# Moving the own part's sums of one batch into a spare column tile of the next batch's decay product

## The chip, the cores and the metric

The kernel runs on one core of a Trainium2 chip. The core has five engines that work side by side, each through its own queue in order: TensorE (PE in the profile; its weight loads are PEld), VectorE (DVE), ScalarE (ACT), GpSimd (POOL), and SyncE (SP), which here issues DMAs. TensorE writes into PSUM, which this kernel uses as eight banks of 128 partitions by 512 fp32 values: six tiles named `ps` and one tile of two banks, `wrep`. The metric is the time of one execution on the device in microseconds; the median of three runs is given.

## The reference

The reference is one block of an RWKV-like layer with 8 batches, 256 time steps, 512 channels, 32 heads of 16 channels. Cut to what matters here:

```
xn  = layernorm(x);  sx = previous row of xn - xn
xxx = tanh((xn + sx * maa_x) @ maa_w1)          # five groups of 32 columns
x5[g] = xn + sx * (maa_stack[g] + xxx[g] @ maa_w2[g])
w = exp(-exp(time_decay + tanh(x5[1] @ decay_w1) @ decay_w2))
r, k, v = x5[3] @ Wr.T, x5[0] @ Wk.T, x5[2] @ Wv.T;  g = silu(x5[4] @ Wg.T)
step t:  a = k_t v_t^T                          # per head, 16 x 16
         out_t = r_t (faaaa * a + s);   s = a + w_t * s
att = groupnorm(out) per head;  x = x + (att * g) @ Wo.T
x = x + sigmoid(xr @ ffn_Wr.T) * (square(relu(xk @ ffn_Wk.T)) @ ffn_Wv.T)
```

In `out_t` the term with `faaaa` needs no state: for each head it is v_t times the sum over the head's channels of faaaa * r_t * k_t. The kernel calls this the own part, and the change is about those sums.

## The kernel before, in words

The work of a batch is written in three stages: `inputs_of_scan` (layer norm, the mixes x5, the decay w, the projections k, v, r, g), `scan` (the recurrence and the own part), and `rest` (group norm, output projection, the feed-forward half). Three batches are in flight: while batch b is in its scan, batch b+1 is in its inputs and batch b-1 in its rest.

Activations lie with channels on partitions and time along the row: a tile of [128, 2, 256] holds two blocks of 128 channels, so one batch of 512 channels takes two tiles (index `q`), four blocks in all.

**The decay product (L785 to L802).** `pd` is one PSUM tile. For each of the four blocks k of the contraction, four matmuls run in the four column tiles of 32 of the array. Tiles 0 and 1 take `decay_w1` (64 columns) with x5[1] as the moving operand. Tiles 2 and 3 take the fifth group of `maa_w1` with `xin`; its 32 columns stand twice in the weight, so tile 3 repeats what tile 2 computes. ScalarE then takes tanh of rows 0 to 63 into `hd` (twice, L800) and of rows 64 to 127 into `tb` (twice, L802), since the next product wants that result repeated on all 128 partitions.

**The own part (L864 to L888).** POOL multiplies r by k into two tiles `rk` (L867). Four matmuls, one per block and column tile, sum them per head with the mask `hm`, which holds faaaa (L872), into 4 x 32 rows of a PSUM tile `pc`. ScalarE copies each block's 32 rows of 256 values onto the four quarters of the tile `att`, 16 copies a batch (L880). POOL multiplies `att` by v (L886).

**The scan (L882 to L936).** For each of the four blocks: DMAs bring v spread over the partitions (`vs`), DVE multiplies by k (L917) and runs the scan (L919), POOL multiplies by r (L922), and a gather of 16 matmul calls on PE (L930) sums over the head's channels into a PSUM tile `pat`. DVE adds `pat` to `att` (L936).

**The other names in the text.** `mul` at L400 issues nearly all other products; a product whose form is "any" runs as four narrow matmuls (128 x 32 of the array) or one wide one (128 x 128), after the form that stood last on PE. L612 is the turn by identity, L754 and L668 additions of POOL in the mixes, L900 the decays for the scan, L989 the copies of the group norm's factors, which take one of the two `rk` tiles for the second half.

**What sets the order.** Every operation is added to a plan with an engine, an estimated time, its tiles and a number. The numbers stand in the long table `TURNS` (from L121), one row a stage: the plan takes the ready operation with the lowest number, gives it a tile of its pool when one comes free, and each engine's queue follows the result. Pools bound the lookahead: six `ps` tiles in PSUM, two `rk`, three `att`, three each of k, r, v, w.

Of the kernel before, what the change touches and what calls it, by code (L numbers as in the profile page):

```python
# [9 lines left out]
AF = mybir.ActivationFunctionType  # L10
ALU = mybir.AluOpType
# [56 lines left out]
class Plan:  # L68
# [46 lines left out]
    def stage(self):  # L115
# [224 lines left out]
def tile_rwkv_block(  # L340
# [357 lines left out]
    def inputs_of_scan(b, got):  # L698
# [102 lines left out]
        for rows in (slice(0, 64), slice(64, 128)):  # L801
            act(T, tb, [pd], lambda rows=rows: nc.scalar.activation(tb()[rows, :], pd()[64:128, 0, :], AF.Tanh), "exp")  # L802
# [354 lines left out]
```

## Time and profile before

| what | value |
|---|---|
| runs, median (lowest to highest) | 609.45 us (609.26 to 609.94) |
| profiled execution, span from first to last instruction | 607.3 us |
| instructions in the trace | 17606 |
| mean granted TensorE clock | 1.000 |
| activation table loads | 43, of 1283 ns each |
| DMA, mean | 205 GB/s |

The profile gives the profiled execution's span, not its device time. The time of a run is about 2 us longer than the span (609.45 - 607.3 = 2.15). A row such as `L872 PE MATMUL ps<-rk,hm 128*32 128x256 f32 x64` reads: line, engine, operation, output from inputs, the form of the array (contraction rows * columns of one tile), the output's shape and type, and the count. An fp32 matmul call appears as two records.

### The profile page before, as it was taken

The page shows a single profiled execution, that of the slowest core. Times are in us where ns is not written, and L with a number is a line of the kernel's source. Part 1 is how long each engine was busy: PE and PEld are TensorE (multiplying, and loading weights), DVE is VectorE, ACT ScalarE, POOL GpSimd, SP SyncE. Part 2 cuts the span into 40 slices and gives each one's busy share as a digit, 9 for nine tenths or more (in the row PEclk, how much of TensorE's full clock was granted, in tenths as well). Part 3 has the DMA queues.
Part 4 walks back from the last instruction along what each step waited for, and adds up shares of the span by engine and source line. Part 5 has one row for each costly group of instructions (what it writes and reads, how often), then busy time and mean ns, then how long its engine had stood idle before and what let it go on. Part 6 is the DMA issues. An engine that isn't in the chain of part 4 may idle for free.

```text
span 607.3 us, 17606 instructions
## 1 busy us (share of the span) xinstructions
PE 597.2 (98%) x7270; PEld 344.8 (57%) x7270; DVE 543.9 (90%) x492; ACT 514.6 (85%) x1172; POOL 520.2 (86%) x417
## 2 busy tenths in 40 slices
PE   9999999999999999999999999999999999999997
PEld 7675555467544664377553775455644464446464
DVE  6699999999999998899989999999999999995442
ACT  6878779999999999999999898999989799965450
POOL 2899999999899999899989998999898998898020
PEclk9999999999999999999999999999999999999999
DMA  8798855878778787859767996688659877951542
GB/s 319 224 266 218 232 147 142 227 181 215 220 220 215 219 219 205 213 145 268 198 198 191 277 239 189 186 240 225 188 174 263 203 204 227 258 186 42 175 168 92
DMA packets 52640, 124.77 MB, mean 205 GB/s; under 512 B 5841, under 2 KB 11345, under 8 KB 52561
## 3 DMA queue, kind: packets, MB, share of 16 engines
q1 hardware_dynamic: 48048, 119.39, 71.3%
q10 hardware_dynamic: 4512, 4.26, 2.3%
q8 instruction: 57, 0.93, 0.7%
q14 instruction: 23, 0.18, 0.1%
HBM read 115.25 MB, written 8.39 MB: 204 GB/s over the span
## 4 chain that ended last, share of the span: by engine, by line
PE 78%; POOL 14%; DVE 3%; issue 3%; ACT 1%; DMA 1%; DVEq 0%; POOLq 0%; ACTq 0%
PE ps L400 65%; PE ps L930 8%; POOL st L922 7%; PE ps L612 2%; POOL mix L754 2%; PE ps L794 2%; POOL vs L914 2%; DVE st L919 1%; POOL mix L782 1%; POOL att L886 1%; POOL sx L640 1%; PE ps L956 1%; DMA xt<-in_x 1%; PE ps L872 0%; DVE vs L917 0%
## 5 line engine op out<-in xcount | busy, mean ns | idle before, releaser
L919 DVE TENSOR_TENSOR_SCAN st<-wrep,vs 128x1024 f32<-128x1024 f32 x128 | 288.2, 2277 | 2.9 <-ACT wrep L900 0.8
L922 POOL TENSOR_TENSOR st<-st,r 128x1024 f32<-128x1024 f32 x128 | 254.5, 2005 | 9.3 <-DVE st L919 9.0
L917 DVE TENSOR_TENSOR vs<-vs,ps 128x1024 f32<-128x1024 f32 x122 | 143.7, 1208 | 2.6 <-ACT vs L910 2.4
L400 PE MATMUL ps<-Ws,mix 128*32 128x512 f32 (+3 forms) x872 | 115.2, 586 | 0.1
L400 PEld LDWEIGHTS ps<-Ws,mix 128*32 128x32 f32 (+1 forms) x872 | 37.6, 116 | 63.4 <-issue 56.0
L754 POOL TENSOR_TENSOR mix<-mix,xn 128x512 f32<-128x512 f32 x62 | 66.6, 1098 | 6.9 <-DVE mix L738 5.5
L930 PE MATMUL ps<-st,con 128*32 128x256 f32 x1024 | 62.1, 380 | 0.8 <-POOL st L922 0.7
L400 PE MATMUL ps<-mix,Wv 128*32 128x256 f32 (+1 forms) x832 | 60.5, 380 | 1.6 <-DVE mix L751 0.9
L400 PE MATMUL ps<-mix,Wk 128*32 128x256 f32 (+1 forms) x952 | 59.2, 379 | 0.1
L400 PE MATMUL ps<-mix,Wg 128*32 128x256 f32 (+1 forms) x664 | 58.8, 379 | 0.0
L400 PE MATMUL ps<-mix,Wr 128*32 128x256 f32 (+1 forms) x688 | 58.5, 380 | 0.0
L400 PE MATMUL ps<-mix,Ws 128*32 128x256 f32 (+1 forms) x664 | 57.3, 379 | 0.0
L400 PE MATMUL ps<-Ws,g 128*32 128x512 f32 (+1 forms) x416 | 56.9, 593 | 0.2 <-POOL g L1001 0.2
L736 ACT ACTIVATE ps<-ps,vec 128x256 f32<-128x256 f32 x112 | 47.6, 444 | 3.8 <-PE ps L400 2.3
L880 ACT COPY att<-ps 32x256 f32<-32x256 f32 x128 | 46.6, 364 | 4.4 <-ACT v L825 1.3
L668 POOL TENSOR_TENSOR mix<-mix,xn 128x512 f32<-128x512 f32 x44 | 47.3, 1093 | 3.4 <-ACT mix L666 3.2
L400 PEld LDWEIGHTS ps<-mix,Wv 128*32 128x32 f32 (+1 forms) x832 | 37.7, 116 | 21.2 <-DVE mix L751 1.6
L400 PEld LDWEIGHTS ps<-mix,Ws 128*32 128x32 f32 (+1 forms) x664 | 40.0, 124 | 15.5 <-ACT o L1025 0.5
L400 PEld LDWEIGHTS ps<-mix,Wr 128*32 128x32 f32 (+1 forms) x688 | 39.3, 123 | 16.5 <-issue 1.3
L930 PEld LDWEIGHTS ps<-st,con 128*32 128x32 f32 x1024 | 32.7, 110 | 27.5 <-issue 4.4
L400 PEld LDWEIGHTS ps<-mix,Wg 128*32 128x32 f32 (+1 forms) x664 | 39.9, 124 | 14.8 <-issue 0.7
L400 PEld LDWEIGHTS ps<-mix,Wk 128*32 128x32 f32 (+1 forms) x952 | 35.0, 112 | 22.3 <-issue 2.9
(141 smaller groups left out, 968.1 us busy)
## 6 DMA issues: line engine op xcount, KB each, us to landing
vs<-vo SPq DMA_DIRECT2D x128, 512.0 KB, 5.7
Ws<-in_fk SPq DMA_DIRECT2D x16, 512.0 KB, 6.1
Ws<-in_wo SPq DMA_DIRECT2D x16, 512.0 KB, 6.2
Ws<-in_fr SPq DMA_DIRECT2D x16, 512.0 KB, 6.1
Ws<-in_fv SPq DMA_DIRECT2D x16, 512.0 KB, 5.2
x<-in_x SPq DMA_DIRECT2D x9, 512.0 KB, 8.0
vo<-v ACTq DMA_DIRECT2D x15, 256.0 KB, 5.4
out<-o SPq DMA_DIRECT2D x15, 256.0 KB, 4.9
```

What stands on the lines that cost most here:

```text
L400: nc.tensor.matmul(out[i : i + n], lhsT=w[:, i : i + n], rhs=x, start=first, stop=final)
L612: nc.tensor.transpose(to[:, m, n * P : (n + 1) * P], xh[n]()[:, k * P : (k + 1) * P], idt())
L668: gp(512, t, [t, xn[q]], lambda q=q, t=t: nc.gpsimd.tensor_tensor(t(), t(), xn[q]()[:, :, 1 : T + 1], ALU.add))
L736: act(256, p_, [p_, vec], lambda g=g, q=q, m=m, p_=p_: nc.scalar.activation(p_()[:, m, :], p_()[:, m, :], AF.Identity, bias=col(f"maa_{g}" ...
L754: gp(512, t, [t, xn[q]], lambda q=q, t=t: nc.gpsimd.tensor_tensor(t(), t(), xn[q]()[:, :, 1 : T + 1], ALU.add))
L794: nc.tensor.matmul(pd()[i : i + 32, 0, :], lhsT=w, rhs=src[k // 2]()[:, k % 2, :], start=(k == begin), stop=(k == end))
L880: act(350, atts[q], [pc], lambda i=32 * (2 * q + m), m=m, q=q, h=32 * h: nc.scalar.copy(atts[q]()[h : h + 32, m, :], pc()[i : i + 32, 0, :]))
L914: gp(4 * T, vs, [vs, k], lambda m=m, vs=vs, k=k: nc.gpsimd.tensor_tensor(vs(), vs(), k.place[:, m : m + 1, 1 : T + 1].to_broadcast([P, 4, ...
L917: dve(4 * T, [vs], [vs, kp], lambda m=m, vs=vs, kp=kp: nc.vector.tensor_tensor(vs(), vs(), kp()[:, m : m + 1, :].to_broadcast([P, 4, T]), ...
L919: dve(4 * T, [st], [w, vs], lambda w=w, vs=vs, st=st: nc.vector.tensor_tensor_scan(st().rearrange("p n t -> p (n t)"), w().rearrange("p n ...
L922: gp(4 * T, st, [st, r], lambda m=m, st=st, r=r: nc.gpsimd.tensor_tensor(st(), st(), r()[:, m : m + 1, :].to_broadcast([P, 4, T]), ALU.mul ...
L930: nc.tensor.matmul(pat()[32 * i : 32 * i + 32, 0, :], lhsT=con()[:, s : s + 32], rhs=done[i]()[:, j, :], start=(j == 0), stop=(j == 3),)
```

## The change

1. In every batch but the first, the fourth column tile of the decay product no longer repeats the third. It runs the own part's matmul of the batch before, one block for each step k: blocks 0 and 1 into rows 96 to 127 of `pd` itself, blocks 2 and 3 into the same rows of a second PSUM tile. The separate product of four matmuls remains only for the last batch.
2. As rows 96 to 127 of `pd` no longer hold the repeated part, `tb` is filled by four tanh of 32 rows instead of two of 64.
3. The two blocks of a tile now lie beside each other on the same 32 partitions, so ScalarE copies them at once: 8 copies of 32 x 512 a batch in place of 16 of 32 x 256. The last batch keeps its 16.
4. The two multiplications r * k on POOL are listed at the end of `inputs_of_scan`, as the next batch's inputs need them; the stages are written down in the order inputs of b+1, scan of b, rest of b.
5. All numbers in `TURNS` are new: 2599 operations instead of 2648.

```
     def inputs_of_scan(b, got):
+        own = gots[b - 1] if b else None
...
                 for k in ks:
-                    for i in range(0, P, 32):
+                    for i in range(0, P if b == 0 else 96, 32):
                         w, src = (dw1()[:, k, i : i + 32], x5[1]) if i < DEC else (w1()[:, k, P + i - DEC : P + i - 32], xin)
                         nc.tensor.matmul(
                             pd()[i : i + 32, 0, :], lhsT=w, rhs=src[k // 2]()[:, k % 2, :], start=(k == begin), stop=(k == end))
+                    if own:
+                        nc.tensor.matmul(own["pc"][k // 2]()[96:128, k % 2, :], lhsT=hm()[:, k, :],
+                                         rhs=own["rks"][k // 2]()[:, k % 2, :], start=True, stop=True)
...
+            if own:
+                own["pc"] = [pd, new("ps", f"pc{b - 1}")]
+                pe(0.432 * len(ks), own["pc"], [dw1, w1, hm, *ins, *own["rks"]], mm, "columns", [hd, tb])
+                continue
             pe(0.432 * len(ks), [pd], [dw1, w1, *ins], mm, "columns", [hd, tb])
...
-        for rows in (slice(0, 64), slice(64, 128)):
-            act(T, tb, [pd], lambda rows=rows: nc.scalar.activation(tb()[rows, :], pd()[64:128, 0, :], AF.Tanh), "exp")
+        n = 32 if own else 64
+        for rows in (slice(i, i + n) for i in range(0, P, n)):
+            act(T, tb, [pd], lambda rows=rows: nc.scalar.activation(tb()[rows, :], pd()[64 : 64 + n, 0, :], AF.Tanh), "exp")
...
+        got["rks"] = []
+        for q in range(NQ):
+            r, k, rk = got["r", q], got["k", q], new("rk", f"rk{b}_{q}")
+            gp(512, rk, [r, k], lambda rk=rk, r=r, k=k: nc.gpsimd.tensor_tensor(rk(), r(), k(), ALU.mult))
+            got["rks"].append(rk)
...
     def scan(b, got):
...
+        if b == NB - 1:
...
+        else:
+            for q, pc in enumerate(got["pc"]):
+                for h in range(0, P, 32):
+                    act(610, atts[q], [pc], lambda q=q, h=h, pc=pc: nc.scalar.copy(atts[q]()[h : h + 32], pc()[96:128]))
...
+    gots = [{} for _ in range(NB)]
+    stages = [(inputs_of_scan, 0, 0)]
     for b in range(NB):
+        stages += [(inputs_of_scan, 0, b + 1)] * (b + 1 < NB) + [(scan, 1, b), (rest, 2, b)]
+    for stage, i, b in stages:
+        stage(b, gots[b])
+        phases[b + i].append((i, plan.stage()))
```

The branch for the last batch holds the code of before; the two lines of `rk` that stood in `scan` are gone there. The new table of numbers is left out.

More of the change, by code (lines that the diff above doesn't have):

```diff
@@ L861, in scan, with mm @@
         act(4, cm, [cm], lambda: nc.scalar.mul(cm(), cm(), -1.0 / S))
-        rks, pc = [], new("ps", f"pc{b}")
-        for q in range(NQ):
-            r, k, rk = got["r", q], got["k", q], new("rk", f"rk{b}_{q}")
-            gp(512, rk, [r, k], lambda rk=rk, r=r, k=k: nc.gpsimd.tensor_tensor(rk(), r(), k(), ALU.mult))
-            rks.append(rk)
-        def mm():
-            for i in range(NK):
-                nc.tensor.matmul(
-                    pc()[32 * i : 32 * i + 32, 0, :], lhsT=hm()[:, i, :], rhs=rks[i // 2]()[:, i % 2, :], start=True, stop=True)
-        atts = [new("att", f"att{b}_{q}") for q in range(NQ)]
-        pe(0.437, [pc], [hm, *rks], mm, "columns")
-        for q in range(NQ):
-            for m in range(2):
-                for h in range(4):
-                    act(350, atts[q], [pc], lambda i=32 * (2 * q + m), m=m, q=q, h=32 * h: nc.scalar.copy(
-                        atts[q]()[h : h + 32, m, :], pc()[i : i + 32, 0, :]))
+        atts = [new("att", f"att{b}_{q}") for q in range(NQ)]
+        if b == NB - 1:
+            pc, rks = new("ps", f"pc{b}"), got["rks"]
+            def mm():
+                for i in range(NK):
+                    nc.tensor.matmul(
+                        pc()[32 * i : 32 * i + 32, 0, :], lhsT=hm()[:, i, :], rhs=rks[i // 2]()[:, i % 2, :], start=True, stop=True)
+            pe(0.437, [pc], [hm, *rks], mm, "columns")
+            for q in range(NQ):
+                for m in range(2):
+                    for h in range(4):
+                        act(350, atts[q], [pc], lambda i=32 * (2 * q + m), m=m, q=q, h=32 * h: nc.scalar.copy(
+                            atts[q]()[h : h + 32, m, :], pc()[i : i + 32, 0, :]))
+        else:
+            for q, pc in enumerate(got["pc"]):
+                for h in range(0, P, 32):
+                    act(610, atts[q], [pc], lambda q=q, h=h, pc=pc: nc.scalar.copy(atts[q]()[h : h + 32], pc()[96:128]))
         for blk in range(NK):
@@ L1073, in tile_rwkv_block @@
     phases[0].append((0, plan.stage()))
+    gots = [{} for _ in range(NB)]
+    stages = [(inputs_of_scan, 0, 0)]
     for b in range(NB):
-        got = {}
-        for i, stage in enumerate((inputs_of_scan, scan, rest)):
-            stage(b, got)
-            phases[b + i].append((i, plan.stage()))
+        stages += [(inputs_of_scan, 0, b + 1)] * (b + 1 < NB) + [(scan, 1, b), (rest, 2, b)]
+    for stage, i, b in stages:
+        stage(b, gots[b])
+        phases[b + i].append((i, plan.stage()))
     with tc.manual_schedule():
```

247 rows, old and new, of the table TURNS are left out of this document.

## The prediction, made before the changed kernel was run

> **What bounds the kernel now.** I read the page's busy times first, then its chain of waits in order of time, then the busy time by stretch. On the page every engine is nearly full, with TensorE (PE) first:
>
> ```profile
> PE 597.2 (98%) x7270; PEld 344.8 (57%) x7270; DVE 543.9 (90%) x492; ACT 514.6 (85%) x1172; POOL 520.2 (86%) x417
> ...
> PE 78%; POOL 14%; DVE 3%; issue 3%; ACT 1%; DMA 1%; DVEq 0%; POOLq 0%; ACTq 0%
> ```
>
> A share of busy time is no bound yet. The chain of waits says where which engine sets the end. Its columns are the start, the length, and the engine with its line:
>
> ```profile
> 34.21 2.00 POOL st L922
> ...
> 48.53 1.05 POOL rk L867
> ...
> 140.21 1.97 POOL st L922
> 142.22 1.93 PE ps L930 x32
> 144.15 3.45 PE ps L400 x64
> ...
> 523.91 3.43 PE ps L400 x32
> 527.34 1.80 PE ps L930 x32
> 529.25 2.15 issue
> 531.40 1.20 DVE vs L917
> ```
>
> So there are three parts. From about 34 to 142 us the chain runs through POOL (the ramp, scans of batches 0 and 1). From 142 to 529 us it runs through PE. The end, from 529 us, is the last batch alone. The busy times by stretch agree and add something (columns: length, then PE, PEld, DVE, ACT, POOL, granted clock, DMA share, GB/s):
>
> ```profile
> 52.00:120.00 68.00, 66.26 (x1121) 37.70 (x1116) 66.71 (x56) 58.21 (x128) 67.95 (x47) 1.00 0.75 187
> 120.00:200.00 80.00, 79.66 (x915) 45.07 (x908) 79.65 (x64) 76.42 (x182) 76.86 (x61) 1.00 0.79 208
> ...
> 360.00:440.00 80.00, 79.91 (x984) 46.09 (x987) 78.45 (x66) 73.37 (x174) 74.97 (x60) 1.00 0.75 207
> 440.00:520.00 80.00, 80.00 (x1164) 41.12 (x1160) 77.94 (x63) 71.81 (x153) 72.99 (x53) 1.00 0.81 218
> ```
>
> From 360 to 520 us PE has 0.09 us idle in 160. VectorE (DVE) has 1.55 and 2.06 us of slack per 80, ScalarE (ACT) 6.63 and 8.19. In the first two rows DVE is as full as PE: 1.29 us of slack in 68, 0.35 in 80. So a microsecond of PE work removed after 142 us should shorten the run by a microsecond, as long as DVE loses less than it has in hand; before 142 us it may buy nothing.
>
> The profiled execution has a span of 607.3 us. The page does not give its device time; the median of the runs is 609.45 us, so I take 2.15 us around the span and hold it fixed.
>
> **Part 1: four matmuls go, seven times (a gain).** The own part's product (L872) has four calls, one per column tile, recorded as eight matmuls. What it takes from PE is the distance from its start to the next group's start:
>
> ```profile
> 52.90 0.61 PE L872 MATMUL ps<-rk,hm 128*32 128x256 f32 x8
> 53.33 1.91 PE L930 MATMUL ps<-st,con 128*32 128x256 f32 x32
> ...
> 96.88 0.61 PE L872 MATMUL ps<-rk,hm 128*32 128x256 f32 x8
> ...
> 182.66 0.61 PE L872 MATMUL ps<-rk,hm 128*32 128x256 f32 x8
> ...
> 390.29 0.61 PE L872 MATMUL ps<-rk,hm 128*32 128x256 f32 x8
> 390.72 3.64 PE L400 MATMUL ps<-mix,Wv 128*32 128x256 f32 x64
> ```
>
> The first and the last pair of rows both give 0.43 us. Batch 7 keeps its product, so seven go: 7 x 0.43 = 3.01 us. The same four calls now run in the fourth column tile of the next batch's decay product (L794), in place of the repeated one. Whether that is free depends on whether a tile with another moving operand runs beside the others. The product of before already mixes two moving operands (with weights from dw and from mw):
>
> ```profile
> 60.24 0.39 PE L794 MATMUL ps<-mix,dw 128*32 128x256 f32 x2
> 60.25 0.39 PE L794 MATMUL ps<-mix,mw 128*32 128x256 f32 x2
> 60.46 0.39 PE L794 MATMUL ps<-mix,dw 128*32 128x256 f32 x2
> ```
>
> All four tiles start within 0.01 us, and the next four 0.22 us later. I therefore cost the replacement at nothing. If the new operand or the second output tile broke this, each of the four steps would cost two further slots of 0.22 us, 1.76 us a batch.
>
> The products of batches 0, 1 and 2 start at 52.90, 96.88 and 182.66 us. So five of the seven (batches 2 to 6) lie in the stretch that PE bounds: 5 x 0.43 = 2.15 us, taken in full. Those of batches 0 and 1 lie in the ramp: between 0 and 0.86 us, and I take half, 0.43, since PE is 97% busy there though not on the chain. Together 2.58 us.
>
> **Part 2: changes of array form (a small loss).** Products without a fixed form run wide (128*128) or narrow (128*32), as the last form in the order was. Counting along the new numbers by that rule I get 82 changes of form on PE against 80 before, and 185 narrow products out of 277 against 186. A change is seen here:
>
> ```profile
> 288.45 3.62 PE L400 MATMUL ps<-mix,Wg 128*128 128x256 f32 x16
> 292.00 0.64 PE L872 MATMUL ps<-rk,hm 128*32 128x256 f32 x8
> 292.46 0.83 PE L400 MATMUL ps<-mix,Wg 128*32 128x256 f32 x12
> ```
>
> Sixteen wide matmuls at 0.216 us would let the next start at 291.91; it starts at 292.00, and the eight narrow ones then take 0.46 instead of 0.43. That is 0.12 us a change, 0.2 us for two.
>
> **Part 3: ScalarE (off the path).** The copies of one batch go from 16 of 32x256 to 8 of 32x512, and the tanh into `tb` from two of 64 rows to four of 32:
>
> ```profile
> L880 ACT COPY att<-ps 32x256 f32<-32x256 f32 x128 | 46.6, 364 | 4.4 <-ACT v L825 1.3 <-PE ps L872 1.3
> L825 ACT COPY k<-ps 128x512 f32<-128x512 f32 x16 | 9.3, 581 | 3.1 <-PE ps L400 3.0
> L802 ACT ACTIVATE tb<-ps 64x256 f32<-64x256 f32 x16 | 6.1, 381 | 0.7 <-ACT v L843 0.4
> L855 ACT ACT_TABLE_LOAD x11 | 14.1, 1283 | 0.2
> ```
>
> No copy of 32x512 is in the trace. The 32x256 and 64x256 rows show that row count hardly matters, so I take 0.58 us from the 128x512 row; the bound above is twice the short one, 0.73, at which the copies gain nothing, and below it is 0.36, that of one short copy. A batch saves 16 x 0.364 - 8 x 0.58 - 2 x 0.381 = 0.42 us, seven save 2.9. Along the new numbers I count 46 changes of the activation table against 43, three more at 1.28 us: 3.9 us. ACT ends about 1 us fuller, of 92.7 us idle. It is 1% of the chain, so I enter nothing; if ACT had no room, that 1 us would be the price.
>
> What a table change costs beside its own row is seen here, where the load starts as the copies end and the next activation starts as it ends:
>
> ```profile
> 55.08 1.28 ACT L855 ACT_TABLE_LOAD   x1
> 56.37 0.60 ACT L855 ACTIVATE g<-ps 128x512 f32<-128x512 f32 x1
> ```
>
> [...]
>
> **Part 4: waits and buffers.** The POOL multiplications into `rk` (L867) are as many as before, only listed at the end of the inputs, and by the numbers they stand where they stood, ahead of the same batch's scan; nothing on POOL gets longer. No DMA is moved by the edit itself, though the new numbers shift SP's loads by four places on average, and I enter nothing for that; a load that came late would show as a wait of PE for a DMA.
>
> The decay product now waits for `rk` of the batch before and for a second PSUM tile. Behind it in PE's queue stands all later work, but `rk` is numbered well before it. What comes later is the result: the copies can only start after the decay product. By the numbers that product stands after the first gather (L930) in batches 2 to 6. Until the copies (4 x 0.58 us), POOL's multiplication by v (L886) and DVE's addition (L936) are done, the gathered tile is held, one of six in PSUM. The waits now are small:
>
> ```profile
> DVE att L936 <- POOL att L886: 3.7, 2, 2.7
> ...
> PEld ps L930 <- POOL st L922: 4.3, 9, 0.9
> ```
>
> Against this stands what is freed. The own part's tile is held today until the last of 16 scattered copies:
>
> ```profile
> 225.55 0.61 PE L872 MATMUL ps<-rk,hm 128*32 128x256 f32 x8
> ...
> 264.72 0.36 ACT L880 COPY att<-ps 32x256 f32<-32x256 f32 x1 [0.44 <-ACT v L825]
> ```
>
> That is 39 us for one tile of six; with eight copies that the numbers put close together, two tiles are held for a shorter time. Which side wins I cannot read from the trace. The bounds are the idle PE time that can go, 1.74 + 0.34 = 2.1 us between 52 and 200 us, and new stalls as priced below. I enter zero.
>
> **The sum.** 2.58 - 0.2 = 2.4 us: span 604.9, time 609.45 - 2.4 = 607.1 us. By itself this case spans 606.4 (all seven products count, no cost of form) to 607.5 (only the five count, 2.15 - 0.2). A measurement of this kernel can tell about 0.2%, 1.2 us, so the forecast is a faster kernel.
>
> **Rivals.** *The order also fills the ramp (0.13).* PSUM is freed sooner and PE's 2.1 us of idle time up to 200 us goes: 609.45 - 3.0 - 2.1 = 604.3 us. For it speaks the 39 us hold; against it that the chain in the ramp is POOL's, whose work stays.
>
> *The gain is hidden (0.17).* The ramp keeps its 0.86 us, and one slot of 0.22 us a batch is given back in PE waits for a PSUM tile, 7 x 0.22 = 1.54 us: 2.15 - 0.2 - 1.54 = 0.4 us, time 609.0. For it: DVE at 79.65 of 80 us up to 200 us. Against: nothing but PE is full after 360.
>
> *Own sums come too late, slower (0.13).* Place: DVE's addition L936, in order, in front of scans that POOL and PE wait for. Today it waits 3.7 us in two cases, 1.85 each. If each of the seven batches waited so, that is 13.0 us, 9.3 more. The four stretches quoted hold 1.29 + 0.35 + 1.55 + 2.06 = 5.2 us of DVE slack, so 4.1 us would reach the end: 609.45 + 4.1 - 2.4 = 611.1 us. It decides from 5.2 + 2.4 = 7.6 us of extra waiting, 1.1 us a batch. Against it: the numbers also move the addition behind more scan work, which is what a wait would need.
>
> *The fourth tile does not run beside the others (0.02).* Then the change doesn't do what it says: 7 x 1.76 - 3.0 = 9.3 us more, 618.8 us. The L794 rows speak against it.
>
> **How the numbers follow.** The forecast has 0.55. Faster is 0.55 + 0.13 = 0.68, within 0.2% 0.17, slower 0.13 + 0.02 = 0.15. The range goes from 604.0, just under the first rival, to 609.9, over the hidden gain with four more such slots; the slower rivals and a small part of the first stay outside, under 0.2.
>
> **What would show it.** Right: L872 with 8 matmul records in place of 64, the decay products still 1.7 us long with four tiles starting together, PE busy about 3 us less and as full as now from 142 us on, a 32x512 copy near 0.58 us. Wrong: matmuls of the fourth tile starting 0.2 us behind the others; DVE's wait for L886 far over 3.7 us; more idle PE time in front of L930 or L400 after 142 us; a chain that leaves PE later than 142 us; or a PE busy time down by 3 us with an equal rise in idle time.

## The result and the profile after

The changed kernel takes 613.65 us (613.19 to 615.54), the kernel before 609.36 us beside it: 1.0075 times as long, interval 1.0059 to 1.0090. It is slower, and outside the range. In two later measurements, on two different chips, the same program came out at 615.88 (1.0105) and 616.64 (1.0115, interval 1.0101 to 1.0129), where the kernel before stayed at 609.26 and 609.50. So the loss is 4.3 to 7.1 us, and it varies where the kernel before does not.

The page of the changed kernel: the busy times, the granted clock in forty slices, and the chain by engine:

```profile
PE 596.3 (97%) x7250; PEld 345.1 (56%) x7250; DVE 542.3 (89%) x492; ACT 511.0 (84%) x1131; POOL 520.0 (85%) x417
...
PEclk9999999899999999999999999999999999999999
...
PE 78%; DVE 10%; ACT 6%; issue 3%; POOL 1%; DMA 1%; DVEq 0%; ACTq 0%; POOLq 0%
```

PE's busy time fell by 0.9 us, not by 3.0, and its idle time rose from 607.3 - 597.2 = 10.1 to 611.7 - 596.3 = 15.4 us. POOL has left the chain (14% before); DVE and ACT have come in, and one of the forty slices has a lower clock. Where the idle time lies is in the stretches (length, PE busy, clock, DMA share, GB/s), first of the kernel before, then of the changed one:

```profile
0.00:52.00 52.00, 49.15 (x542) 1.00 0.87 263
```

```profile
0.00:52.00 52.00, 48.08 (x486) 1.00 0.87 261
52.00:120.00 68.00, 62.16 (x1085) 0.99 0.75 196
```

Idle time grew by 49.15 - 48.08 = 1.1 us up to 52 us and from 1.74 to 5.84 us between 52 and 120. Nearly all 5.3 us of new idle time lie before 120 us.

A milestone shows it without windows. Before its ninth gather each kernel has done the same work but for the products of batches 0 and 1. That gather and the last one (the 32nd), before and changed; a gather is one row of 32 records:

```profile
175.75 1.91 PE L930 MATMUL ps<-st,con 128*32 128x256 f32 x32
...
555.16 1.93 PE L930 MATMUL ps<-st,con 128*32 128x256 f32 x32
```

```profile
180.07 1.91 PE L954 MATMUL ps<-st,con 128*32 128x256 f32 x32
...
559.13 1.93 PE L954 MATMUL ps<-st,con 128*32 128x256 f32 x32
```

The changed kernel is 4.3 us late at the ninth gather and 4.0 at the last. From one to the other it takes 379.1 us against 379.4, although five products (2.15 us of matmuls) are gone there. So two questions: what is lost in the start, and where the 2.15 us went.

The product itself does what the prediction said. Two of the four steps of a decay product:

```profile
101.70 0.41 PE L804 MATMUL ps<-mix,dw 128*32 128x256 f32 x2
101.74 0.38 PE L804 MATMUL ps<-mix,mw 128*32 128x256 f32 x1
101.75 0.38 PE L807 MATMUL ps<-rk,hm 128*32 128x256 f32 x1
101.92 0.41 PE L804 MATMUL ps<-mix,dw 128*32 128x256 f32 x2
```

The fourth tile with its own operand starts 0.01 us behind the third, and the next four 0.22 us behind the first. The replacement is free.

The chain of waits shows the start, and one stretch in the middle, leaving PE (start, length, what):

```profile
51.10 7.98 DMA vs<-vo
...
94.80 2.29 DVE st L943
...
113.51 4.46 DVE st L943 x2
...
121.99 11.71 PE ps L409 x136
...
311.37 1.02 ACT wrep L924
...
337.70 1.06 POOL att L910
...
348.12 2.17 issue
350.29 2.33 DVE vs L941 x2
353.00 10.63 PE ps L409 x48
```

In the kernel before, the chain from 142 to 529 us is PE alone. Now ACT, POOL and DVE carry it from 309 to 353 us, where by this chain shorter PE work should buy nothing. In the start it goes through a DMA of the state copies and DVE's scans.

Three waits of the start stand out. First, POOL's queue at 30 to 43 us:

```profile
33.51 1.09 POOL L877 TENSOR_TENSOR rk<-r,k 128x512 f32<-128x512 f32 x1 [1.65 <-ACT r L843]
...
41.09 2.38 POOL L938 TENSOR_TENSOR vs<-vs,k 128x1024 f32<-128x1024 f32 x1 [1.33 <-ACT vs L934]
```

POOL idles 3.0 us there, behind `rk` and then `vs`. Before, its longest wait in this place was 0.22 us. Second, ACT waits for a copy that DMAs bring:

```profile
59.11 0.30 ACT L934 ACTIVATE vs<-s,cm 128x4 f32<-128x4 f32 x1 [3.05 <-DMA vs<-vo]
```

Between 49.84 and 55.71 us SP now issues loads of `x` and of `Wo` between the four copies. In the kernel before, six copies stand there without a load. Third, PE waits for PSUM tiles and for what fills them, and then runs at half clock (rows, then the stretches, which end with clock, DMA share and GB/s):

```profile
116.04 0.71 PE L409 MATMUL ps<-tb,mw2b 32*128 32x256 f32 x8 [1.80 <-ACT r L843]
118.56 3.43 PE L954 MATMUL ps<-st,con 128*32 128x256 f32 x32 [1.81 <-DVE mix L787]
```

```profile
114.00:116.00 2.00, 0.23 (x7) 1.00 0.66 205
116.00:118.00 2.00, 0.71 (x8) 1.00 0.44 80
118.00:120.00 2.00, 1.44 (x17) 0.71 0.94 258
120.00:122.00 2.00, 2.00 (x24) 0.50 0.72 180
122.00:124.00 2.00, 2.00 (x20) 0.94 0.43 147
```

A gather of 32 matmuls takes 3.43 us here and 1.91 at 180.07 us. The clock lost over these three stretches is 2 x (0.29 + 0.50 + 0.06) = 1.7 us.

My theory was that the new order makes the start wait, and that the removed PE work does not reach the end. The rivals: the new form itself makes the waits; the loss is spread over the run; the removed work is worth its 3 us and only covers a larger loss.

### The profile page after: what moved, and what is told of

Read it like the earlier page. It is cut to its first block, busy times and chain, and to the rows that moved or that the text cites. A ratio compares the mean times of both kernels' runs of the same rounds, so it can differ in the third digit from the quotient of the medians.

```text
span 611.7 us, 17524 instructions
## 1 busy us (share of the span) xinstructions
PE 596.3 (97%) x7250; PEld 345.1 (56%) x7250; DVE 542.3 (89%) x492; ACT 511.0 (84%) x1131; POOL 520.0 (85%) x417
## 4 chain that ended last, share of the span: by engine, by line
PE 78%; DVE 10%; ACT 6%; issue 3%; POOL 1%; DMA 1%; DVEq 0%; ACTq 0%; POOLq 0%
PE ps L409 64%; PE ps L954 8%; DVE st L943 4%; PE ps L621 2%; DVE vs L941 2%; ACT ps L746 2%; PE ps L804 1%; DMA vs<-vo 1%; DVE mix L748 1%; PE ps L532 1%; ACT rk L1013 1%; POOL st L946 1%; PE ps L980 1%; ACT sq L1013 0%; DVE mix L670 0%
## 5 line engine op out<-in xcount | busy, mean ns | idle before, releaser
L409 PEld LDWEIGHTS ps<-mix,Wk 128*32 128x32 f32 (+1 forms) x856 | 36.5, 115 | 22.1 <-issue 2.0
L746 ACT ACTIVATE ps<-ps,vec 128x256 f32<-128x256 f32 x112 | 45.3, 443 | 2.1 <-PE ps L409 1.0
L934 ACT ACTIVATE vs<-s,cm 128x4 f32<-128x4 f32 x128 | 36.4, 296 | 10.4 <-DMA vs<-vo 9.4
```

The costliest lines, as they stand in the source:

```text
L409: nc.tensor.matmul(out[i : i + n], lhsT=w[:, i : i + n], rhs=x, start=first, stop=final)
L746: act(256, p_, [p_, vec], lambda g=g, q=q, m=m, p_=p_: nc.scalar.activation(p_()[:, m, :], p_()[:, m, :], AF.Identity, bias=col(f"maa_{g}" ...
L934: act(4, vs, [s0, cm], lambda i=i, blk=blk, vs=vs: nc.scalar.activation(vs()[:, :, 0:1], s0()[:, blk, 4 * i : 4 * i + 4].rearrange("p (n o ...
```

## The experiments

"Fourth gather" and so on count from the first. A run's time is a median, its ratio is to the kernel before on the same chip.

**Form and order apart.** First the new form with the numbers of before, then the old form with the new numbers.

```
 TURNS = """
-        3 66 7 11 25 71 31 62
+        1 69 8 22 53 86 91 104
...
```

> The changed kernel's code with the order numbers of the kernel before: every operation that both have keeps its old number, the decay product keeps its own, the eight copies take every second old copy number, the four tanh the two old ones. Theory 1 (the new numbers cost it, in the first 120 us; the new form itself saves PE work): about 607 us, 2 to 3 us below the kernel before at 609.4. Theory 2 (the new form costs it, by two PSUM tiles that are held for the own sums): 611 us or more, slower than before, with PE waits where four tiles are asked for at once.

672.77 us (1.1039, interval 1.1008 to 1.1069). The waits at 345 to 406 us (sum, count, longest):

```profile
DVE att L962 <- POOL att L912: 11.6, 1, 11.6
...
ACT att L907 <- PE ps L809: 9.4, 1, 9.4
...
POOL att L912 <- ACT att L907: 6.7, 1, 6.7
```

The old order had the own sums long before the next decay product. Tied to that product, they come late, and PE, ACT, POOL and DVE wait in turn. This is the mechanism of the slower rival, at its full price: with these old numbers the new form cannot be had. Other numberings near the old ones were not tried.

```
-                    for i in range(0, P if b == 0 else 96, 32):
+                    for i in range(0, P, 32):
...
+        pe(0.437, [pc], [hm, *rks], mm, "columns")
```

> The kernel before with the order numbers of the changed kernel: the own part's product stands just before the next decay product, its 16 copies at the numbers of the eight. Theory 1: as slow as the changed kernel or slower by its 3 us of PE work, 613 to 617 us, with the loss before 120 us. Theory 2: near 610 us, since the form that costs is not there.

618.52 us (1.0147, interval 1.0131 to 1.0164). The old form is slow in the new order too, and slower than the changed kernel in any of its three measurements. On the chip where the changed kernel took 615.88 us it is 2.6 us over it, near the 3.0 us of the product that it still has. So the loss comes with the order, not with the form.

**The product taken out of the old order.** Own sums of batches 0 to 6 are left out but for one matmul of 32 columns; then the same for batches 2 to 6 alone.

```
-            for i in range(NK):
+            for i in range(NK if b == NB - 1 else 1):
+                n = T if b == NB - 1 else 32
```

> The kernel before, its order untouched, with the own part's product of batches 0 to 6 cut from four matmuls of 256 columns to one of 32 (the own sums are left out, most of PSUM tile pc stays unwritten). What it saves is only PE work, about 0.35 us a batch, 2.4 us in seven. If PE work is worth its full time after 142 us, as the prediction had it: 1.7 to 2.4 us faster, 607 to 607.7 us. If the waits between the engines take it back: under 0.6 us, 609.

> The kernel before, in its own order, with the product of the own sums cut to one matmul of 32 columns in batches 2 to 6 alone (so these own sums are left out of the output); batches 0 and 1 keep it. The prediction took these five in full: 5 x 0.43 = 2.15 us less, 607.2 us. Theory 1 (PE's waits take most of the saving back wherever it lies, as the cut of all seven gave 1.2 us for 2.9): about 608.2 to 608.9 us.

608.21 us (0.9978, interval 0.9969 to 0.9988) and 608.89 us (0.9985, interval 0.9977 to 0.9994), each beside a kernel before of 609.35 and 609.72. The one short matmul that stays costs little: at 390 us a product and the 64 records behind it take 394.36 - 390.29 = 4.07 us in the kernel before, and 394.92 - 391.24 = 3.68 us with the sums left out. That is 0.39 us a batch (0.30 in the first), so about 2.6 us for seven and 1.9 for five. Of these 2.6 us, 1.1 arrive (0.7 to 1.9 by the interval), and of the 1.9 us, 0.8 (0.4 to 1.4). Also in the old order a removed PE microsecond arrives in part only, by the medians less than half of it. The ninth and the last gather with the five left out:

```profile
176.64 1.91 PE L931 MATMUL ps<-st,con 128*32 128x256 f32 x32
...
555.72 1.93 PE L931 MATMUL ps<-st,con 128*32 128x256 f32 x32
```

They are 379.1 us apart, against 379.4 before.

**The product put back into the new order.** Four more matmuls stand behind each decay product, into rows that nothing reads.

```
+                if own:
+                    for i in range(0, P, 32):
+                        nc.tensor.matmul(
+                            own["pc"][1]()[i : i + 32, 1 if i < 96 else 0, :],
...
```

> The changed kernel, its order untouched, with four more matmuls of the own part's form behind each decay product of batches 1 to 7 (they repeat one block and write three unused ones): the 0.43 us of PE work that the change took out, put back. If the saving is real and only covered by the loss at the start: about 2 to 3 us slower than the changed kernel. If it had no worth: within 0.6 us of it.

616.75 us (1.0123, interval 1.0100 to 1.0146). Against the first measurement of the changed kernel that is 3.1 us more, and I read it as PE setting the pace. The next measurement of the same changed program was 615.88, which leaves 0.9. The question went to one chip, below.

**One half of the run in each order.** Old form and old numbers up to the seventh gather, the new ones behind it; then the reverse.

```
-        own = gots[b - 1] if b else None
+        own = gots[b - 1] if b > 2 else None
...
```

> A mixture: form and numbers of the kernel before up to the third gather of batch 1 (about 142 us), form and numbers of the changed kernel after that, so the own sums of batches 2 to 6 are in the spare tile. If the loss of the changed kernel is made in its start: about 609 us, 4 to 5 us faster than the changed kernel, and level with or up to 2 us below the kernel before. If it is made by the new form anywhere: 612 us or more.

> The kernel of the change up to the seventh gather (146.7 us of its trace): new form and new turns for batches 0 and 1; behind it the old form and the old turns. Theory 1 (the loss lies in the new order of the start, and the rest of the run gains nothing): the seventh gather comes at 146 to 147 us, as in the changed kernel and 4.5 us later than before, and what follows takes as long as before, so 609.4 + 5.4 less the streamed work of two products (0.86 us), about 613.5 to 614.5 us. Rival (the loss lies in the new order as a whole, a little in each stretch): the start carries only half of the 4.3 us and the total is 611 to 612 us. A junction between two orders can add some us of waits of its own just behind the seventh gather, which the trace would show there.

With the old start, 613.03 us (1.0064, interval 1.0046 to 1.0081); with the new start, 620.95 us (1.0179, interval 1.0165 to 1.0193). Both totals miss what I expected if the start makes the loss (about 609, and 613.5 to 614.5 us), and taken alone the first fits the rival. The traces show why I do not count them: where the two orders meet, both lose. Old start:

```profile
142.43 1.93 PE L955 MATMUL ps<-st,con 128*32 128x256 f32 x32 [0.32 <-POOL st L947]
...
156.25 3.57 PE L955 MATMUL ps<-st,con 128*32 128x256 f32 x32 [2.12 <-ACT xn L645]
```

New start:

```profile
148.71 1.93 PE L955 MATMUL ps<-st,con 128*32 128x256 f32 x32
...
157.57 0.33 PE L622 MATMUL ps<-idt,xh 128*128 128x128 f32 x1 [3.48 <-ACT xh L602]
...
187.92 1.91 PE L955 MATMUL ps<-st,con 128*32 128x256 f32 x32
```

The seventh gather comes at 142.22 us in the kernel before and at 146.75 in the changed one; the old start gives 142.43, the new one 148.71. That part is told apart. The totals are not, since the junctions add waits of their own. Behind the ninth gather, the new start with the old rest needs 619.4 - 187.92 = 431.5 us to the end of its span, the kernel before 607.3 - 175.75 = 431.6, the changed one 611.7 - 180.07 = 431.6: the rest of the run is equal in all three. It is not in the profile of the old start: from 142.43 to its ninth gather at 179.68 us it takes 37.25 us against 33.53 before (the junction), and from there to the end 613.6 - 179.68 = 433.9 us, 2.3 more than the others. That profile is the slowest of its eight runs (615.38 us, lowest 611.12), and what lengthens it there stays open.

**What a stall of POOL costs in the start.** The kernel before runs its first product r x k four times.

```
-            gp(512, rk, [r, k], lambda rk=rk, r=r, k=k: nc.gpsimd.tensor_tensor(rk(), r(), k(), ALU.mult))
+            gp(512, rk, [r, k], lambda rk=rk, r=r, k=k, n=4 if (b, q) == (0, 0) else 1: [
+                nc.gpsimd.tensor_tensor(rk(), r(), k(), ALU.mult) for _ in range(n)][-1])
```

> The kernel before with its first POOL product r times k (32.90 us) run four times in place of once: 3 x 1.05 us more of POOL at that place, the results the same, the order the same. Theory 1 (POOL sets the pace from 30 to 142 us, so that 3 us lost there are lost for good, as in the changed kernel): the seventh gather comes 2.5 to 3.3 us later than the 142.2 us of before and the time is about 612 to 612.6 us. Rival (POOL's lost time is made up behind it): the seventh gather is less than 1 us later and the time is under 610.3 us.

```profile
33.69 4.61 POOL L868 TENSOR_TENSOR rk<-r,k 128x512 f32<-128x512 f32 x4
```

4.61 us in place of 1.09, 3.5 more; the time is 613.29 us (1.0057, interval 1.0042 to 1.0073), 3.6 more. POOL sets the pace at that place of the kernel before, and a stall of it arrives whole.

**The waits of the start repaired one after the other.** The numbers stay; single operations are moved in the finished order. First the three loads a little later, behind the copy `vs0_3_0`:

```
+        late = [op for op in ops if op.engine == "DMA" and op.bufs[0].name in ("x21", "Wo0_0", "Wo0_1")]
...
+        for op in ops[: at + 1] + late + ops[at + 1 :]:
```

> The changed kernel with only three DMA issues moved in SP's order: the second x tile and both halves of Wo of batch 0, from between the spread loads of v near 50 us to behind the last spread load of batch 0's fourth block. If their bytes make the loads of v land late (the wait of 3 to 4 us near 59 us) and this starts the loss: 1.5 to 3 us faster than the changed kernel, that wait under 1 us and the second gather's stretch without PE loss. If not: the same time.

613.94 us (1.0070, interval 1.0054 to 1.0086). The wait of 3.05 us falls to 1.39, another of 2.7 us for a state copy comes at 84 to 99 us, and the fourth gather stays at 97.8 us. Beside the first measurement of the changed kernel nothing is gained. Beside its second, 615.88 us on the same chip as this run, 1.9 us are, with intervals that just overlap. Then POOL's gaps as well:

```
+        move(is_("ACT", "xin1_1"), is_("ACT", "vs0_0_2"), 0)
+        move(is_("POOL", "xin1_1"), is_("POOL", "rk0_0"), 0)
+        move(is_("POOL", "vs0_1_3"), is_("POOL", "st80_0_1"), 1)
```

> The changed kernel with three DMA issues moved as in the run with the loads behind, and two repairs on POOL's path between 30 and 44 us: ScalarE's two mix operations of line 675 that feed POOL's line 677 go ahead of the decay and the state weights, so that POOL can run that mix ahead of rk, and POOL's state product of the second scan goes ahead of the product with k that waits for ScalarE. Theory 1 (POOL is the bound of the start, and its 3.0 us of idle time at 30 to 42 us come out at the end): POOL idles 1 us there in place of 3, the fourth gather comes at about 95.8 us in place of 97.8, and the time is about 612 us against 613.9. Rival (the time is given back at the waits for PSUM tiles and buffers that follow): the fourth gather comes earlier but the sixth or seventh doesn't, and the time stays at 613.5 to 614.5 us.

614.60 us (1.0072, interval 1.0054 to 1.0090), fourth gather at 97.2. The chain at 50 to 100 us shows a likely reason why 2 us of POOL brought 0.6:

```profile
75.30 11.93 DMA vs<-vo
```

This copy takes 11.93 us from issue to landing, against a median of 5.4 us on the changed kernel's page; the moved loads were issued from 71.21 us on, shortly ahead of it. So they go to a quieter place at 96 us (DMA share in this profile 0.72 from 94 to 100 us and 0.37 from 100 to 106, against 1.04 and 1.06 from 70 to 82):

```
-        move(is_("DMA", "x21", "Wo0_0", "Wo0_1"), is_("DMA", "vs0_3_0"), 1)
+        move(is_("DMA", "x21", "Wo0_0", "Wo0_1"), is_("DMA", "vs1_0_0"), 1)
```

> The repaired start (POOL without gaps) with the three loads x21, Wo0_0 and Wo0_1 behind the copy vs1_0_0, at about 96 us, where the DMA share is 0.3 to 0.4, in place of at 71 us; x21 is read at 192 us and Wo at 121 us. In the trace of the run before, the chain of 50 to 100 us has one DMA vs<-vo of 11.93 us (75.30 to 87.23) for which ScalarE waits 2.64 us and after it VectorE and TensorE. Theory 1 (these waits are what kept the repair of POOL from coming out): the wait of 2.6 us goes, the fourth gather comes at 95 us (97.2 before), and the time is 612 to 612.8 us. Rival (the start has so many nearly equal chains that the next wait takes its place): the fourth gather at 97 us, and 614 to 615 us as before.

613.37 us (1.0064, interval 1.0039 to 1.0090). The fourth gather comes at 95.9 us, 1.9 before the changed kernel's, but the fifth at 117.7 against 118.6: most is given back between the two. Last, ACT's copies of v, k and r right behind their products. In this run three copies of the group norm's factors moved too far: POOL multiplies by these factors at 112.10 and 113.15 us, ahead of the copies at 113.24 and 114.29, so the group norm of batch 0 lacks a part of its factors, and POOL is spared its wait for them.

```
+        move(lambda op: op in filler, is_("ACT", "r2_0"), 1)
+        move(is_("ACT", "v2_0", "k2_1"), is_("ACT", "wrep1_1"), 0)
```

> The same, and ScalarE's copies of v, k and r of batch 2 (114.4 to 116.0 us in the changed kernel), which free three of the six PSUM tiles, go ahead of one weight replication and of the last three copies of line 1013, each right behind its product; nothing else moves. Theory (PE's wait of 1.8 us for PSUM tiles at 114 to 116 us, and the half clock that follows it, come from ScalarE's order): the wait falls to about 0.7 us and the fifth gather comes 1 us earlier than in the run with the loads far behind, and if the half clock goes too, 1.7 us more: 1 to 2.7 us less than that run. Rival (the gather waits for the mix on VectorE and POOL, not for the tiles): no change.

613.92 us (1.0090, interval 1.0071 to 1.0108), fifth gather at 117.6: no change. PE's wait behind ACT's copy of r falls from 2.60 us to 0.76, and its wait for the mix grows from 1.25 to 3.86. The chain at 98 to 118 us:

```profile
105.83 3.97 POOL st L946 x2
109.79 2.37 POOL vs L938
112.16 2.11 POOL att L1016 x2
...
115.12 1.59 ACT att L1020 x3
```

So PSUM tiles were not what held the fifth gather: POOL's queue was, then ACT's, in which the mix for the gather stands behind the group norm of the batch before. An earlier try of the same step, by renumbering, delayed the copies instead:

> The changed kernel with three ScalarE copies of batch 2 (of v, k and r, at 114.4 to 116 us in its profile) numbered right behind the products that they empty, ahead of sixteen copies of the group norm's factors. If the second part of the loss is PE's wait for a PSUM tile at 114 us and the half clock behind it (1.8 + 1.8 us of waits and 1.7 us of clock): 610 to 611.5 us and no stretch at half clock. If DVE sets the pace there and PE only waits for it: under 1 us faster, 613 us, with the wait moved.

618.46 us (1.0157, interval 1.0138 to 1.0176): ACT waited 1.8 us for PE and PE 3.8 us for the mix. Another renumbering, meant to delay the loads, left the program as it was:

> The changed kernel with three loads numbered later, as in the kernel before: the two halves of Wo of batch 0 and the second x tile of batch 1, which the new numbers issue between the spread loads of v near 50 us. Theory 1, if the late landings of v (ACT waits 3.05 us for one at 59 us) make the first part of the loss: 611 to 612 us, 1.5 to 2.5 us faster than the changed kernel, and that wait under 1 us. If the loads are not it: no change, 613.6 us.

Its 615.88 us (1.0105, interval 1.0085 to 1.0124) is a second measurement of the changed kernel, and it showed that my comparisons across chips were worth less than I had taken them for.

**Four kernels on one chip.** The changed kernel, the one with the repaired start (POOL's gaps and the loads far behind), and each of them with the product put back.

> The changed kernel as it is, on the chip of the next two: the yardstick for them. From its two measurements so far (1.0075 and 1.0105 of before) 613.5 to 616 us. No theory is told apart by it alone.

> The changed kernel with POOL's two gaps filled and the three loads far behind, beside the changed kernel on one chip. Theory 1 (the waits repaired at 30 to 98 us, which brought the fourth gather 1.9 us and the seventh 0.5 us forward in the traces, come out at the end): 1 us or more under the changed kernel. Rival (later waits and the half clock take it back): within 0.7 us of it.

> The changed kernel with the four matmuls of the product put back behind each decay product, beside the changed kernel on one chip. If TensorE bounds the new order, 7 x 0.43 = 3.0 us over the changed kernel. If the new order hides TensorE work as the old order does (1.2 us gained for 2.9 us less), about 1.2 us over it.

> The kernel with the repaired start (1.0064 and 1.0057 of before on two chips), with the four matmuls of the product put back behind each decay product: 7 x 0.43 = 3.0 us more work for TensorE. If TensorE bounds the repaired order, 3.0 us over it, 1.0106 of before, about 616 us. If the removed work is hidden behind the waits of the other engines there as well, as in the changed kernel on one chip (615.79 with the product, 616.64 without), 613 to 614.2 us.

| kernel | us (lowest to highest) | ratio to before, interval | ninth gather | ninth to last gather |
|---|---|---|---|---|
| changed | 616.64 (616.09 to 617.09) | 1.0115, 1.0101 to 1.0129 | 182.01 | 380.2 |
| changed, product back | 615.79 (615.22 to 616.80) | 1.0103, 1.0090 to 1.0117 | 179.57 | 382.3 |
| repaired | 613.00 (612.61 to 613.25) | 1.0057, 1.0043 to 1.0070 | 179.58 | 378.6 |
| repaired, product back | 615.00 (613.53 to 616.41) | 1.0099, 1.0083 to 1.0116 | 177.84 | 381.5 |

The times are medians of four or five runs; the two columns of gathers come from one profile of each kernel. The repairs are worth 3.6 us on this chip, half of the loss. What they removed is seen in the waits at 26 to 100 us, changed and then repaired:

```profile
ACT vs L934 <- DMA vs<-vo: 6.5, 3, 4.6
DVE vs L941 <- ACT vs L934: 4.8, 2, 3.0
```

```profile
ACT vs L934 <- DMA vs<-vo: 3.9, 3, 2.0
...
DVE vs L941 <- ACT vs L934: 2.3, 2, 1.8
```

In the first trace of the changed kernel the longest such wait was 3.1 us, here 4.6. That fits the differences between chips, which the repaired kernel (613.37 and 613.00) does not show; whether the chip makes the difference was not tried by itself.

Between the changed kernel and its partner the intervals overlap: with the start unrepaired, putting 3.0 us of PE work back costs nothing that can be told. In the repaired kernel it costs 2.0 us by the medians, and the intervals lie apart, though the five runs with the product scatter from 613.53 to 616.41 us. Behind the ninth gather the product costs 2.0 and 2.9 us, for 2.15 us of matmuls: there PE does set the pace of the new order. Ahead of it the kernels with the product are 2.4 and 1.7 us earlier. PE's queue ahead of the fifth gather tells what to make of that, first with the product back, then the same kernel in its earlier run on the other chip:

```profile
116.48 0.71 PE L409 MATMUL ps<-tb,mw2b 32*128 32x256 f32 x8 [1.43 <-ACT r L848]
119.19 1.93 PE L959 MATMUL ps<-st,con 128*32 128x256 f32 x32 [1.99 <-DVE mix L787]
```

```profile
116.88 0.71 PE L409 MATMUL ps<-tb,mw2b 32*128 32x256 f32 x8 [1.45 <-ACT r L848]
119.58 3.64 PE L959 MATMUL ps<-st,con 128*32 128x256 f32 x32 [1.98 <-DVE mix L787]
```

The waits are the same, 4.1 us with 0.71 us of work in them. Once the gather runs at full clock, once at half. So the half clock is a matter of the run, not of the product: in its four runs on this chip that kernel had a mean clock of 1.000 twice and of 0.997 twice. In the four profiles of this chip the two with the product happen to lack it. It explains only a part of the 2.4 and 1.7 us. The changed kernel on this chip, without the product:

```profile
105.88 3.66 PE L409 MATMUL ps<-mix,Wk 128*32 128x256 f32 x64 [0.85 <-ACT v L843]
...
120.73 3.40 PE L954 MATMUL ps<-st,con 128*32 128x256 f32 x32 [1.77 <-DVE mix L787]
```

Where the fifth gather starts, before a matmul has run at half clock, the kernels with the product already lead by 120.73 - 119.19 = 1.5 us and 118.07 - 116.92 = 1.2 us. The two without it wait 0.85 and 1.49 us for ACT's copy of v ahead of the product with Wk, and the two with it do not. The repaired kernel waited only 0.34 us there in its earlier profile, so this wait varies between runs of one program. With one profile of each kernel it stays open whether the product does anything in the start.

Of my theory, the first half holds: the new order makes the start wait, and what the repairs removed arrived at the end. The second holds for the changed kernel, where the removed work is hidden behind those waits, but no longer for the repaired one, where 2.0 of 3.0 us arrive.

## Why the prediction was wrong

**The product and its replacement: right.** The fourth tile starts with the others, and the separate product's records go from 64 to 8. The removed work is 3.0 us.

**The five products taken in full: wrong in the sum.** In the old order they are worth 0.3 us between the ninth and the last gather (379.1 us with the five left out, 379.4 before) and 0.8 at the end. In the new order they are worth 2.0 to 2.9, but with them that order needs 381.5 to 382.3 us where the old one needs 379.4. The new order costs there what the removed work saves; which wait takes it was not isolated. The busy row of PE, 0.09 us idle in 160, had misled me. With 1.9 us left out of the old order between these gathers, PE's busy time there falls by 1.0 us only (378.30 to 377.33), and its idle time grows by 0.6 (1.11 to 1.75). So a part of the removed time turned into idle time, and a part into rows that take longer and count as busy. One place in the start shows how: at 97.31 us eight matmul records of L956 take 1.17 us, all of it counted as busy, where such a row takes 0.61 at 221.66. With the product of that batch left out, four of the eight wait 0.32 us for ACT, and the decay product behind them starts 1.25 us after the own part's product either way (98.13 - 96.88 before, 98.30 - 97.05 without): nothing is gained there.

**Half for the two in the ramp: not borne out.** No gain of 0.43 us is seen in the start; the waits and the half clock, which vary there from run to run, are larger than that.

**"I enter zero" for waits and buffers: the step that failed.** "the new numbers shift SP's loads by four places on average, and I enter nothing for that" is the part of it that the runs bear out best: the loads stand between the state copies, and with POOL's two gaps they make 2.4 us at the ninth gather and 3.6 at the end on the chip where both were measured. Moving the loads alone brought 1.9 us on another chip, just at the edge of the intervals; POOL's gaps were not filled by themselves. Where the prediction entered zero, PE's idle time grew by 5.3 us in the first profile, 5.2 of it before 120 us. I looked at tiles of PSUM and at PE's wait for a DMA; the wait came at ACT and reached PE by way of DVE and POOL. I had read that POOL sets the pace up to 142 us, and did not follow the new numbers along POOL's own queue.

**ScalarE: right in effect, small in size.** The copy of 32x512 takes 0.579 us, as taken (0.58). Table loads went from 43 to 44, not to 46, and ACT is 3.6 us less busy in place of 1 more. The 0.2 us for changes of form were not tried; no run here can tell so little.

**The rivals.** "Own sums come too late" had the right sign and the wrong place. `DVE att L960 <- POOL att L910` is 0.4 us in all in the changed kernel; with the old numbers it was 31.2 us. None of the rivals was a start that waits for its loads.

**What stays open.** The repaired kernel is still 3.5 us over the kernel before, 3.8 at the ninth gather. It waits at 100 to 120 us behind POOL and ACT and then has the half clock (0.50 from 119 to 122 us in its last profile); that an order without this exists was argued from the kernel before, not shown. That the decay product's tile is held longer was not tried by itself. No version here beats the kernel before; even with the product of seven batches simply left out, its order is only 1.1 us faster.

## What to carry to other kernels

A new order is a change by itself, and in a start where every queue is full it can cost more than the work it was made for saves (here 4.3 to 7.1 us against 3.0): follow it along each queue, first that of the engine which sets the pace, then that of the DMAs. To size work taken off a full engine, take it out in the old order first; here that gave 1.1 of 2.6 us. Measure the changed kernel and its variants on one chip when the change makes waits for DMAs: the changed program took 613.65, 615.88 and 616.64 us in three measurements here.

## What the runs showed of the hardware that was not expected

In eight profiles of the changed order and its variants TensorE was granted half the clock around the fifth gather, which in seven of them stands behind 4.1 to 5.3 us that hold only 0.71 us of matmuls (in the eighth, behind 5.1 us with 1.24). From the granted clock of the stretches I estimate that it lasted 3.4 us in four of them (the changed kernel in its first and last measurement, the repaired one on the last chip, ACT's copies moved) and 6.8 us in the other four (the second measurement of the changed kernel, the product put back at first, the loads a little later, the loads at 96 us). The gather of 32 matmuls took 3.00 to 3.64 us there in place of 1.93. In two profiles with like waits, the two with the product put back on the last chip, the clock stayed at 1.00. What decides it was not shown: waits of 1.45 and 1.98 us around the 0.71 us of matmuls once came with the half clock, 1.43 and 1.99 us did not. Nor does the clock always fall at the gather. In the first run with the loads at 96 us its mean was 1.00 from 112 to 114 us and 0.73 from 114 to 116; if it went from 1.00 to 0.50 at once, it fell at about 114.9 us, 2.3 us after the last matmul had ended at 112.61.

A state copy of 512 KB landed after 5.4 us in the median, after 7.98 us on the changed kernel's chain and, in one case, after 11.93 us shortly behind three loads. That the loads delayed it was not tried apart from the other repairs.
